# A decoder's state-space scans, prepared by halves and beside the first attention

## The chip, the cores and the metric

The kernel runs on one core of one Trainium2 chip. A core has five engines with a queue of instructions each: TensorE (PE, matmuls and transposes; PEld is its loading of weights), VectorE (DVE), ScalarE (ACT), GpSimd (POOL) and SyncE (SP, which issues the DMA transfers). Each engine works through its own queue in order; engines wait for one another through semaphores. The metric is the device time of one execution in microseconds (us).

## The reference

A decoder of four layers works on `x` of 4 x 256 x 256 (batch, positions, width), with a context of 4 x 256 x 128. Each layer is three parts, and after each part comes `x = layernorm(x + part(x))`: twelve parts in all. The change touches the first six at most:

- **First attention** (16 query heads of 128 that share one key and value head, causal, rotary positions).
- **First state-space part.** Its scan depends on the *context* alone; `x` only enters through the gate:

```python
x = jnp.einsum('ed,bld->bel', in_proj_w, hidden_states)   # the context
xc = conv of 4 taps over the positions of x, per channel
u = silu(xc + conv_b)
dt, Bm, Cm = split(x_proj_w @ u)                          # 8, 16 and 16 rows
delta = softplus(dt_proj_w @ dt + dt_proj_b)
state = state * exp(delta * A) + (delta * u) * B_t        # 16 states, 256 positions
y = sum over states of state * C_t, + D * u
out = y * silu(z)                                         # z is the decoder's x
```

- **First feed-forward part ("thought").** The last position of each batch is normed, multiplied by `agg_w`, and goes four times through norm, a 256x1024 matmul, gelu and a 1024x256 matmul. The result is broadcast over the positions, weighed by `sigmoid(x @ gate_w + gate_b)`, added and normed.
- **Second attention** (16 query heads of 16, four key heads), **second state-space part** (of the same form as the first), then a mixture of 32 experts and six more parts.

## The kernel before

`x` is held in SBUF as [128, 8, 256] (8 tiles of 128 positions) and also transposed, `xT`. The parts run one after the other in one program. A scheduler in the build decides the order in each engine's queue from the order in the source, from tile buffers and from priorities, so the order in a queue isn't the source's; the orders spoken of below are read from the built programs.

Since the scans of both state-space parts need only the context, they run beside other parts. `Scans` is a generator. `begin(pre)` starts it for layer "l0x" or "l1x" and runs its preparation, `beside(n)` issues n scan steps, `upto(b)` as many as batch b needs. One layer has 4 batches x 16 states = 64 scan steps over [128, 2, 256], two layers 128. One step issues: a broadcast DMA of B and C for the state (`bc`, 256 KB); two exponentials `dA<-delta,negA` on ACT; the product `s<-du,bc` on POOL (L123); the scan `s<-dA,s` on DVE (L520); the product with C, `s<-s,bc`, on DVE (L111); and one matmul that adds up the states into a PSUM bank, `ssmps<-s,idz` on PE. `s` and `bc` have four buffers, the scans have one PSUM bank ("ssmps"), and this bank serves the preparation too.

The preparation of a layer (`_steps` up to `turn = 0`) is: load the four taps of the convolution and multiply them with the input projection (POOL); four banks of convolution matmuls; Silu over all 2048 columns; for each half (two batches) a matmul to `xd`, two DMAs to `bcd` in DRAM, two matmuls of `dt` with an add on DVE (`delta<-ssmps`) and an Abs on ACT (`du<-ssmps`); then Exp and Ln over all 2048 columns, and for each of two channel halves `delta<-delta,du` on DVE (L120) and `du<-delta,u` on POOL.

The first attention, `run_mqa`, has 32 steps n, 8 for each batch. A step issues `shares(n)` (reciprocals and scaling of the weights p), `scores(n+1)`, `queries(n+4)` (into the bank `pm`, tag "mm"), two scan steps, `turn(n)` (transposes of p), `output(n-1)` (acc<-oT) and `sums(n)` (o and oT). After the eighth step of a batch the accumulator is added to x (`x<-acc`), and the norm follows. `gate_pair(b)` finishes the first state-space part for one batch: Silu of x, product with y, two transposes, add to x, norm.

`run_thought` prepares its weights, makes the gates (8 pairs of matmuls and one Sigmoid), runs the chain of the last positions and the loop of four turns (each with one `rstd<-ps`), reads the result (`lastmean`), and goes through the gated tail. `run_gqa` is the second attention: 8 projections with one scan step each, then 32 steps of `SmallHeads.run` with one each.

Of the kernel before, what the change touches and what calls it, by code (L numbers as in the profile page):

```python
# [231 lines left out]
def run_mqa(K, w, more):  # L232
    nc, tc = K.nc, K.tc
    with ExitStack() as ctx:
# [121 lines left out]

        N = 8 * B
        keys(0)
# [9 lines left out]
        for n in range(N):  # L368
            shares(n)
            if n + 1 < N:  # L370
                scores(n + 1)
            if n + 4 < N:
                queries(n + 4)
            if n in (2, 3, 4, 5):
                rest.pop(0)()
            if n == 6:
                more()
            K.scans.beside(2)
            turn(n)
            if n:  # L380
                output(n - 1)
            sums(n)
            if n % 8 == 2 and n > 8 and K.fused(0):
                gate_pair(K, wk, y, n // 8 - 1)
        output(N - 1)
        if K.fused(0):
            gate_pair(K, wk, y, B - 1)
            K.scans.begin("l1x")
# [9 lines left out]
class Scans:  # L398
    def __init__(self, K, ctx):
        tc = K.tc  # L400
        self.K = K
        self.one = ctx.enter_context(tc.tile_pool(name="ssm1", bufs=1))
        self.wk = ctx.enter_context(tc.tile_pool(name="ssm2", bufs=4))
        self.ps = ctx.enter_context(tc.tile_pool(name="ssmp", bufs=1, space=PSUM))
        self.dram = ctx.enter_context(tc.tile_pool(name="ssmd", bufs=2, space=bass.MemoryType.DRAM))

        self.dA = [self.one.tile([P, DC, L], F32, name=f"dA{k}") for k in range(3)]
        for t in self.dA:
            K.nc.gpsimd.memset(t[:, :, 0:1], 0.0)
        self.w = {}  # L410
        self.left = iter(())
        self.done = 0

# [12 lines left out]
    def begin(self, pre):  # L426

        self.left = self._steps(pre)
        self.done = 0
        next(self.left)  # L430
# [11 lines left out]
    def _steps(self, pre):  # L442
        K, nc, w, wk = self.K, self.K.nc, self.w[pre], self.wk
        cols = w["cols"]
        N = B * L
        u = self.one.tile([P, DC, N], F32, name="u", bufs=2)
        delta = self.one.tile([P, DC, N], F32, name="delta")
        du = self.one.tile([P, DC, N], F32, name="du")
# [3 lines left out]
        for j in range(4):  # L452
            t = wk.tile([P, D], F32, name="tap", tag="bc", padded_shape=[P, 2 * L])
            nc.sync.dma_start(out=t, in_=K.A[f"{pre}_cw"][:, j * D : (j + 1) * D].to_broadcast([P, D]))
            K.ptt(t, t, w["in"], MUL)
            taps.append(t)
        for h in range(2):
            for c in range(DC):
                ps = self.bank()
                for j in range(4):  # L460
                    K.mm(ps, taps[j][:, c * P : (c + 1) * P], K.ctxp[:, 2 * h : 2 * h + 2, j : j + L], j == 0, j == 3)
                K.act(u[:, c, 512 * h : 512 * h + 512], ps, AF.Identity, bias=cols[:, c, 0:1])
        K.act(u, u, AF.Silu)
        negA = self.one.tile([P, DC, 16], F32, name="negA")
        K.act(negA, cols[:, :, 2:18], AF.Exp)
        K.ts(negA, negA, -1.0, None, MUL)
        bc = self.dram.tile([2, 16, N], F32, name="bcd")
        for h in range(2):
            s = slice(512 * h, 512 * h + 512)
            xd = wk.tile([P, 512], F32, name="xd", tag="s")  # L470
            ps = self.bank()
            for c in range(DC):
                K.mm(ps[0:40, :], w["xp"][:, c, :], u[:, c, s], c == 0, c == DC - 1)
            nc.scalar.copy(xd[0:40, :], ps[0:40, :])
            for k in range(2):
                nc.sync.dma_start(out=bc[k, :, s], in_=xd[8 + 16 * k : 24 + 16 * k, :])
            for c in range(DC):
                ps = self.bank()
                K.mm(ps, w["dt"][:, c * P : (c + 1) * P], xd[0:8, :])

                K.ts(delta[:, c, s], ps, cols[:, c, 1:2], None, ADD)
                K.act(du[:, c, s], ps, AF.Abs, bias=cols[:, c, 1:2])
        K.act(du, du, AF.Exp, scale=-1.0)
        K.act(du, du, AF.Ln, bias=K.eps[1.0])
        for c in range(DC):
            K.stt(delta[:, c, :], delta[:, c, :], 0.0, du[:, c, :], MAX, ADD)
            K.ptt(du[:, c, :], delta[:, c, :], u[:, c, :], MUL)

        turn = 0
        self.y = u  # L490
# [4 lines left out]
        def add(b, n, s):  # L495
# [4 lines left out]
            if n == 15:  # L500
                for c in range(DC):
                    v = u[:, c, b * L : (b + 1) * L]
# [3 lines left out]
        for b in range(B):  # L506
            lo = b * L
            for n in range(16):
                yield
                if len(late) > 1:  # L510
                    add(*late.pop(0))
                t = wk.tile([P, 2, L], F32, name="bc", tag="bc")
                nc.sync.dma_start(out=t, in_=bc[:, n, lo : lo + L].unsqueeze(0).to_broadcast([P, 2, L]))
# [20 lines left out]
def gate_pair(K, pool, y, b):  # L534

    K.scans.upto(b)
# [3 lines left out]
    K.ptt(gate, gate, y[:, :, b * L : (b + 1) * L], MUL)  # L540
# [7 lines left out]
def run_gate(pre):  # L548


    def run(K, w, more):
# [3 lines left out]
        with ExitStack() as ctx:  # L555
            wk = ctx.enter_context(K.tc.tile_pool(name="gate1", bufs=2))
            ctx.enter_context(K.turns())
            for b in range(B):
                gate_pair(K, wk, y, b)
# [25 lines left out]
def run_thought(K, w, more):  # L585
# [4 lines left out]
    with ExitStack() as ctx:  # L590
# [82 lines left out]

        gate = one.tile([P, NT, D], F32, name="gate")
        for i in range(NT):
            ps = pm.tile([P, D], F32, name="ps", tag="mm")
            for c in range(DC):
                K.mm(ps, K.xT[:, c, i * P : (i + 1) * P], w["gate"][:, c, :], c == 0, c == DC - 1)
            K.tt(gate[:, i, :], ps, row["gate_b"], ADD)
        K.act(gate, gate, AF.Sigmoid)  # L680

# [15 lines left out]
        ct = centred(th, B)  # L697

# [49 lines left out]
        K.scans.beside(24)  # L748
# [233 lines left out]
def run_gqa(K, w, more):  # L982
    nc, tc = K.nc, K.tc
    more()
    with ExitStack() as ctx:
# [46 lines left out]
        if K.fused(3):  # L1032
            heads16.then = lambda b: gate_pair(K, wk, K.scans.y, b)
# [1404 lines left out]
```

## Time and profile before

| | |
|---|---|
| median of 3 runs | 2505.26 us (2502.23 to 2517.76) |
| profiled execution | 2505.99 us, its span 2504.2 us |
| mean granted PE clock | 0.939 |
| PE, DVE, ACT, POOL busy | 2277.2, 1460.8, 802.4, 530.6 us |
| first scan, last scan of the second layer | 88.6 and 771.4 us |
| last x<-acc of the first attention | 393.7 us |
| first rstd of the thought loop, lastmean | 442.2 and 519.6 us |
| last norm of the thought's tail | 567.7 us |
| first exponential, last norm of the second attention with its gates | 623.1 and 799.4 us |

Times in the profile are counted from the span's start. A line of a timeline has the start, the duration in us, the engine, the line of the kernel, the operation, output<-inputs, their shapes and the count; in brackets stands the idle time of the engine just before it and what ended it. Line numbers can be those of a helper (L111 is `tt`, L115 `ts`, L120 `stt`, L123 `ptt`, L126 `act`, L132 `mm`). The table of windows gives busy time and, in brackets, the number of instructions for each engine, then the granted PE clock, the share of the DMA engines and GB/s. The page's slices are 40 equal parts of the span, each digit the busy share in tenths.

### The profile page before, as it was taken

To read this page: it belongs to the slowest core of one execution; us is meant where nothing else is said; L and a number is where in the kernel's file an instruction comes from. 1 tells how busy PE (TensorE), PEld (TensorE's weight loads), DVE (VectorE), ACT (ScalarE), POOL (GpSimd) and SP (SyncE) were. 2 spreads that over 40 slices of the span, in tenths; PEclk is the share of its full clock that TensorE was granted. 3 is DMA by queue.
4 is the path that set the end of the run, shared out by engine and by line. 5 is a ranking of instruction groups with operands and counts; after the bars stand their busy time and mean duration, and the time that the engine had idled before them with its cause. 6 is when DMAs were issued, how large, how long until landed. Compare 5 with 4: busy or idle time off the path is not lost. (4 is left out here: it accounts for less than half of the span.)

```text
span 2504.2 us, 28859 instructions
## 1 busy us (share of the span) xinstructions
PE 2277.2 (91%) x10624; PEld 1526.3 (61%) x10624; DVE 1460.8 (58%) x2824; ACT 802.4 (32%) x1781; POOL 530.6 (21%) x617
## 2 busy tenths in 40 slices
PE   8798988648996999989999999999999989799997
PEld 5466654224443565545888888888776544476774
DVE  3798984588875412182356454444555667774556
ACT  3566663422442111153111111111122244343434
POOL 2544543663332222210001100011110002100001
PEclk9899999677987999999999999999988899999999
DMA  5221221122223254230123111211100002100000
GB/s 197 60 60 45 57 54 40 41 61 42 52 46 109 88 158 130 66 112 29 45 66 110 48 58 45 71 46 47 46 22 1 20 18 70 40 1 1 1 1 17
DMA packets 132836, 138.99 MB, mean 56 GB/s; under 512 B 13876, under 2 KB 120726, under 8 KB 130904
## 3 DMA queue, kind: packets, MB, share of 16 engines
q1 hardware_dynamic: 132696, 137.16, 19.1%
q8 instruction: 84, 1.38, 0.2%
q14 instruction: 56, 0.46, 0.1%
HBM read 134.27 MB, written 2.85 MB: 55 GB/s over the span
## 5 line engine op out<-in xcount | busy, mean ns | idle before, releaser
L132 PE MATMUL ps<-xw,xcT 128*128 128x256 f32 (+1 forms) x2304 | 519.0, 382 | 0.3 <-ACT YT L126 0.3
L132 PEld LDWEIGHTS ps<-xw,xcT 128*128 128x128 f32 x2304 | 430.7, 190 | 64.2 <-issue 1.9
L132 PE MATMUL sc<-kT,qT 32*128 32x256 f32 (+2 forms) x1024 | 240.7, 412 | 11.1 <-DVE qn L129 10.7
L520 DVE TENSOR_TENSOR_SCAN s<-dA,s 128x512 f32<-128x512 f32 x128 | 210.3, 1666 | 35.6 <-POOL s L123 35.4
L123 POOL TENSOR_TENSOR s<-du,bc 128x512 f32<-128x512 f32 x128 | 178.9, 1410 | 231.0 <-PE ssmps L132 191.1
L132 PEld LDWEIGHTS sc<-kT,qT 128*128 128x128 f32 (+1 forms) x1024 | 152.9, 206 | 92.3 <-issue 57.8
L132 PE MATMUL ssmps<-s,idz 128*128 128x512 f32 x256 | 147.1, 683 | 33.6 <-DVE s L111 33.5
L111 DVE TENSOR_TENSOR xp<-ps,xb 128x256 f32<-128x256 f32 x96 | 40.4, 421 | 227.0 <-PE ps L132 224.8
L126 ACT ACTIVATE dA<-delta,negA 128x255 f32<-128x255 f32 x256 | 117.7, 501 | 160.5 <-DVE s L520 160.3
L126 ACT ACTIVATE p<-sc,nm 128x256 f32<-128x256 f32 (+1 forms) x256 | 112.1, 445 | 109.5 <-DVE nm L129 103.7
L111 DVE TENSOR_TENSOR hT<-u,a 128x512 f32<-128x512 f32 x48 | 33.2, 691 | 186.1 <-PE u L132 186.1
L132 PE MATMUL o<-pT,vt 128*128 128x256 f32 (+1 forms) x352 | 121.1, 467 | 21.9 <-ACT pT L332 21.5
L123 POOL TENSOR_TENSOR xp<-xp,rn 128x128 f32<-128x128 f32 x96 | 35.2, 402 | 476.9 <-DVE rn L1406 476.9
L169 POOL TENSOR_SCALAR rstd<-mv 128x2 f32<-128x2 f32 x48 | 12.2, 255 | 551.3 <-DVE mv L161 541.4
L126 ACT ACTIVATE sq<-xp 128x1024 f32<-128x1024 f32 x24 | 25.4, 1057 | 314.3 <-DVE xp L111 314.2
L129 DVE TENSOR_REDUCE qn<-sc 128x2 f32<-128x480 f32 (+1 forms) x192 | 87.2, 506 | 43.6 <-PE sc L132 42.9
L129 DVE TENSOR_REDUCE nm<-sc 128x2 f32<-128x512 f32 (+1 forms) x128 | 77.2, 613 | 49.8 <-PE sc L132 49.2
L126 ACT ACTIVATE e<-sT 128x512 f32<-128x512 f32 x128 | 70.1, 591 | 108.3 <-PE sT L132 107.8
L1474 DVE TENSOR_TENSOR_SCAN dec<-xT,idz 128x256 f32<-128x256 f32 (+1 forms) x192 | 89.8, 537 | 25.0 <-DMA xT<-ad 25.0
L111 DVE TENSOR_TENSOR s<-s,bc 128x512 f32<-128x512 f32 x128 | 103.6, 829 | 1.1
L123 POOL TENSOR_TENSOR hT<-hT,sel 128x512 f32<-128x512 f32 x48 | 60.7, 1268 | 202.1 <-DVE hT L111 102.6
L132 PE MATMUL sT<-q,kT 32*128 32x256 f32 (+1 forms) x384 | 96.4, 502 | 1.7 <-ACT e L126 1.5
(503 smaller groups left out, 4067.1 us busy)
## 6 DMA issues: line engine op xcount, KB each, us to landing
bc<-bcd SPq DMA_DIRECT2D x128, 256.0 KB, 4.6
xw<-in_l2a_xw_dram SPq DMA_DIRECT2D x24, 768.0 KB, 4.9
xT<-ad SPq DMA_DIRECT2D x12, 1024.0 KB, 4.5
wj<-in_l1f_gate_dram SPq DMA_DIRECT2D x48, 128.0 KB, 2.6
wj<-in_l1f_up_dram SPq DMA_DIRECT2D x48, 128.0 KB, 3.1
wj<-in_l1f_down_dram SPq DMA_DIRECT2D x48, 128.0 KB, 3.5
sel<-cwd SPq DMA_DIRECT2D x32, 192.0 KB, 3.0
sel<-cwd SPq DMA_DIRECT2D x32, 128.0 KB, 3.5
```

The source lines that it names most:

```text
L111: self.nc.vector.tensor_tensor(out=out, in0=a, in1=b, op=op)
L123: self.nc.gpsimd.tensor_tensor(out=out, in0=a, in1=b, op=op)
L126: self.nc.scalar.activation(out, in_, func, **kw)
L129: self.nc.vector.tensor_reduce(out=out, in_=in_, axis=AX.X, op=op, **kw)
L132: self.nc.tensor.matmul(out, lhsT=lhsT, rhs=rhs, start=start, stop=stop)
L169: self.nc.gpsimd.tensor_scalar(out=out, in0=in_, scalar1=add, scalar2=None, op0=ADD)
L520: nc.vector.tensor_tensor_scan(out=s.rearrange("p c l -> p (c l)"), data0=dA.rearrange("p c l -> p (c l)"), data1=s.rearrange("p c l -> p ...
L1474: nc.vector.tensor_tensor_scan(out=dec[:, k, h, :], data0=ap[:, h, at(bb, k, j) : at(bb, k, 2)], data1=K.idz[:, 0 : (2 - j) * P], initial=0.0,
```

## The change

The preparation becomes a generator of its own, `prepare(pre, bank)`, with 13 yields, which goes by halves of two batches: each half has its own tiles u, delta and du, and its chain is run to its end before the second half's begins. Silu is applied to each bank of the convolution, Exp and Ln to each half. The product du = delta * u moves from POOL to DVE. The taps get tiles of their own, one buffer each, which both layers use. The first layer's preparation uses the scans' bank as before. The second layer's uses the attention's bank "mm", and three of its pieces are issued in each of the attention's last four steps; the rest follows the last `output`. After that eight scan steps are issued, and 32 instead of 24 ahead of the thought's tail. The gates of the first three batches come at n % 8 == 5 instead of 2. In `run_thought` the gates' matmuls come after the chain's start. `upto` moves from `gate_pair` to its callers.

```diff
@@ run_mqa
         N = 8 * B
+        bank = lambda: pm.tile([P, 512], F32, name="ps", tag="mm")
+        ahead = K.scans.prepare("l1x", bank)
...
             sums(n)
-            if n % 8 == 2 and n > 8 and K.fused(0):
-                gate_pair(K, wk, y, n // 8 - 1)
+            if K.fused(0):
+                if n % 8 == 5 and n > 8:
+                    gate_pair(K, wk, y, n // 8 - 1)
+
+                if n + 4 >= N:
+                    for _ in range(3):
+                        next(ahead)
         output(N - 1)
         if K.fused(0):
+            K.scans.upto(B - 1)
+            for _ in ahead:
+                pass
+            K.scans.start("l1x")
             gate_pair(K, wk, y, B - 1)
-            K.scans.begin("l1x")
+            K.scans.beside(8)
@@ Scans
     def begin(self, pre):
-        self.left = self._steps(pre)
+        for _ in self.prepare(pre, self.bank):
+            pass
+        self.start(pre)
...
-    def _steps(self, pre):
+    def prepare(self, pre, bank):
...
-        u = self.one.tile([P, DC, N], F32, name="u", bufs=2)
-        delta = self.one.tile([P, DC, N], F32, name="delta")
-        du = self.one.tile([P, DC, N], F32, name="du")
...
         for j in range(4):
-            t = wk.tile([P, D], F32, name="tap", tag="bc", padded_shape=[P, 2 * L])
+            t = self.one.tile([P, D], F32, name=f"tap{j}")
...
         for h in range(2):
+            u, delta, du = (self.one.tile([P, DC, 2 * L], F32, name=n, bufs=3) for n in ("u", "delta", "du"))
+            halves.append((u, delta, du))
             for c in range(DC):
-                ps = self.bank()
+                ps = bank()
                 for j in range(4):
                     K.mm(ps, taps[j][:, c * P : (c + 1) * P], K.ctxp[:, 2 * h : 2 * h + 2, j : j + L], j == 0, j == 3)
-                K.act(u[:, c, 512 * h : 512 * h + 512], ps, AF.Identity, bias=cols[:, c, 0:1])
-        K.act(u, u, AF.Silu)
+                K.act(u[:, c, :], ps, AF.Silu, bias=cols[:, c, 0:1])
+            yield
...
+                K.ts(delta[:, c, :], ps, cols[:, c, 1:2], None, ADD)
+                K.act(du[:, c, :], ps, AF.Abs, bias=cols[:, c, 1:2])
+            yield
+            K.act(du, du, AF.Exp, scale=-1.0)
+            K.act(du, du, AF.Ln, bias=K.eps[1.0])
+            yield
+            for c in range(DC):
+                K.stt(delta[:, c, :], delta[:, c, :], 0.0, du[:, c, :], MAX, ADD)
+                K.tt(du[:, c, :], delta[:, c, :], u[:, c, :], MUL)
+                yield
-        for c in range(DC):
-            K.stt(delta[:, c, :], delta[:, c, :], 0.0, du[:, c, :], MAX, ADD)
-            K.ptt(du[:, c, :], delta[:, c, :], u[:, c, :], MUL)
@@ run_thought
-        gate = one.tile([P, NT, D], F32, name="gate")
-        for i in range(NT):
-            ps = pm.tile([P, D], F32, name="ps", tag="mm")
-            ...
-        K.act(gate, gate, AF.Sigmoid)
-
         last = K.tp.tile([B, D], F32, name="last", tag="tp")
...
         ct = centred(th, B)
+
+        gate = one.tile([P, NT, D], F32, name="gate")
+        for i in range(NT):
+            ...
+        K.act(gate, gate, AF.Sigmoid)
...
-        K.scans.beside(24)
+        K.scans.beside(32)
```

## The prediction

> **What bounds the kernel now.** I read the page's slices first, because the change touches only the first layer and the start of the second: from the experts of the second layer on, each engine's instruction order is the same in both built programs.
>
> ```profile
> PE   8798988648996999989999999999999989799997
> DVE  3798984588875412182356454444555667774556
> ```
>
> A slice is 62.6 us. TensorE (PE) is 80 to 90% busy nearly everywhere; its two low stretches in the first 800 us are slices 7 to 9 (438 to 563 us), the thought loop and its gated tail. VectorE (DVE) is nearly full in slices 3 to 5, half empty in slices 1, 7 and 8. So two engines take turns as the bound, and the scans, which are DVE work, are the load that can be moved. Next, a table of windows cut at the kernel's own marks: first scan, last x<-acc of the attention, first rstd of the thought loop, lastmean, last norm of the tail, first exponential and last norm of the second attention.
>
> ```profile
> core 0: us, PE busy (x) PEld busy (x) DVE busy (x) ACT busy (x) POOL busy (x), PEclk, DMA share, GB/s
> 88.00:394.00 306.00, 267.42 (x1096) 182.38 (x1097) 265.12 (x340) 186.32 (x529) 150.12 (x108) 0.94 0.22 54
> 394.00:442.00 48.00, 40.75 (x142) 21.09 (x141) 19.63 (x42) 18.49 (x26) 20.21 (x39) 0.89 0.18 45
> 442.00:520.00 78.00, 47.62 (x223) 19.77 (x223) 52.64 (x51) 40.32 (x70) 45.89 (x33) 0.72 0.24 54
> 520.00:568.00 48.00, 19.13 (x46) 9.65 (x47) 40.68 (x85) 7.51 (x17) 29.73 (x33) 0.65 0.20 45
> 568.00:623.00 55.00, 49.83 (x193) 27.79 (x193) 46.05 (x90) 13.36 (x36) 20.18 (x38) 0.78 0.23 48
> 623.00:799.00 176.00, 156.52 (x971) 71.74 (x967) 128.98 (x191) 70.90 (x133) 53.38 (x53) 0.87 0.23 53
> ```
>
> In the first attention both engines are close to full (267 and 265 of 306 us). In the tail DVE is the bound (40.7 of 48), in the second attention PE (156.5 of 176). Between 394 and 442 DVE works only 19.6 of 48 us. The DVE timeline says why: no scan is ready.
>
> ```profile
> 382.87 0.69 DVE L111 TENSOR_TENSOR s<-s,bc 128x512 f32<-128x512 f32 x1
> ...
> 393.69 0.76 DVE L111 TENSOR_TENSOR x<-acc,x 128x256 f32<-128x256 f32 x2 [6.12 <-PE acc L132]
> ...
> 458.25 2.36 DVE L120 SCALAR_TENSOR_TENSOR delta<-delta,du 128x1024 f32<-128x1024 f32 x2 [9.45 <-ACT du L126]
> ...
> 467.37 2.27 DVE L520 TENSOR_TENSOR_SCAN s<-dA,s 128x512 f32<-128x512 f32 x1 [1.00 <-POOL s L123]
> ```
>
> The 64th scan's product ends at 383.6 and the 65th scan starts at 467.4: 84 us in which the second layer's scans are being prepared (394 to 465, 71 us) and none runs. The 46 left after the thought loop (128 scans less the 82 ahead of lastmean) lie in the tail, the projections and the second attention, where they compete for the bound.
>
> **The change, part by part.** The profiled execution took 2505.99 us (span 2504.2), the median is 2505.26; I sum against 2506.
>
> *One scan step* costs DVE 1.666 us (mean of 128 scans, 1.185 to 2.298) and 0.829 for the product with C, PE one 512-column matmul. On PE,
>
> ```profile
> 358.51 1.88 PE L132 MATMUL ssmps<-s,idz 128*128 128x512 f32 x4
> 360.23 0.60 PE L330 MATMUL ps<-idz,p 128*128 128x128 f32 x4
> ```
>
> four records are two matmuls, 1.72 us between the starts, so 0.86 us each. Beside the second attention the same matmul takes 0.96 to 1.12 us.
>
> *What the orders say.* By the count of scans ahead of each mark on DVE, before and after: last x<-acc 64 and 65; first rstd 64 and 81; lastmean 82 and 106; end of the tail 88 and 110; the second attention gets 29 before and 15 after, the 15 inside its first half. So the move does take place; the question is what each window pays.
>
> *First scan.* It waits for half a preparation instead of a whole one. Before: products of delta at 80.3, then 5.6 us of POOL for du, first scan at 88.6. After, by the same rows shifted: first half's delta at about 62, but the four tap products for the second layer now stand on POOL ahead of the first s, behind the second half's convolution (65) and a 2.9 us DMA; with 4 x 0.72 and s at 1.3 the scan starts near 73.5. The 15 us are not all gain: 6.4 us of DVE work that stood ahead of the first scan now stands behind it.
>
> *Last x<-acc of the attention, 393.7 before.* DVE's bound: 265.1 + 6.4 + one more scan and product 2.5 + the second preparation 8.0 (four adds of 0.75, four 0.6, four products of 0.65 that POOL had) = 282 us of work; with the 33 to 41 us of waits that this window has now, 73.5 + 282 + 33..41 = 388 to 397. The attention's own bound: step 28's o matmul stands at 364.3; with three scans fewer ahead of it and one gate put off I place it at 350. From there to the last x<-acc before took 28.3; the preparation puts 24 matmuls into it, 24 x 0.86 = 20.6, and 3 us of waits: 52, so 402. The later bound holds: **402 (+8)**, ends 388 and 412.
>
> This is where eight more table loads fall into ACT's queue (23 before in the first two layers, 37 after: Silu, Exp and Ln now change by halves between the attention's exponentials). They are in the 52 at nothing beyond the 3 us, because ACT works 186 of 306 us here; queued behind a load are the step's Exp, then its transposes, o and oT. The row:
>
> ```profile
> 431.56 0.69 ACT L126 ACTIVATE du<-ssmps,w_l1x_cols 128x512 f32<-128x512 f32 x1 [2.29 <-DVE delta L115]
> 432.26 1.28 ACT L126 ACT_TABLE_LOAD   x1
> 433.56 1.91 ACT L126 ACTIVATE gate<-gate 128x2048 f32<-128x2048 f32 x1
> ```
>
> A load is 1.28 us and the next activation starts 0.02 us after it. Uncovered, eight cost 8 x 1.28 = 10 us; that is the upper end, 412. The Trainium skill speaks against the change here: "ScalarE: Activation LUTs", section "What ACT_TABLE_LOAD costs", prices a switch of tables at the load plus a drain of about the same length, some 2.66 us. The row shows the load and no such drain around it. By the page, an estimate, eight uncovered switches would be 21 us and x<-acc would come near 423; I go by the row.
>
> *x<-acc to first rstd, 48.5 before.* DVE had 19.6 us of work here; now it gets 16 scans, 16 x 2.5 = 40, with the rest 61.3. At 0.92 busy, as in the attention's undisturbed steps (18.6 of 20 us), 66; ends 62 (full) and 72 (0.85, the tail's share). The eight pairs of gate matmuls leave for the time behind the first chain, which is hidden by PE's idle time (7 of 48 here, 30 of 78 in the loop). **66 (+17.5)**: the new scans stand in front of the loop's start.
>
> *Thought loop, 77.4 before.* 25 scans instead of 18, but preparation (delta, du; 3.0 + 2.4) and waits gone: DVE 64.6 at 0.9, **72 (-5)**. Its chain of small matmuls and norms needs its own time; two of its four turns take 18.3 and 17.8 us with scans beside them, 4 x 17.5 = 70 is the lower end.
>
> *Tail, 48.1 before:* DVE 40.7, of which 7 scans; after 4, 7.5 us less, and 1.5 of waits: **39 (-9)**.
>
> *Projections, 55.4:* DVE 46 with 9 scans, 33 with 3 or 4; PE works 49.8 at a clock of 0.78, of which 6 scans' matmuls: **44 (-11)**, PE's bound.
>
> *Second attention, 176.3:* PE at 0.89 is the bound. 14 or 15 scans fewer, 0.96 to 1.12 us of PE and, where DVE holds the pair of steps, 1.91 us of DVE: 14 x 0.96 = 13 to 15 x 1.91 = 29. I take 1.3 for each, nearer to PE, **157 (-19)**; ends 166, as DVE has slack in the half without scans, and 147.
>
> The marks become 402, 468, 540, 579, 623, 780, against 393.7, 442.2, 519.6, 567.7, 623.1, 799.4. The last mark comes 19 us earlier and nothing behind it changes: 2506 - 19 = **2487**.
>
> **Rivals.** *The preparation hides in the last four steps.* For: PE idles 13% of the window, ACT 39%. Against: both bounds lie above 388. Then x<-acc at 388 (-14 from mine) and, with scans ready sooner, the second attention at 150 (-7): 2466.
>
> *The one bank in the last four steps holds up the attention (slower).* Attention and preparation share one PSUM bank and ACT's in-order queue. Each of the 12 fills must be read by ACT before the next, while a step's queue waits. The preparation alone took 71 us in 394 to 465; if nothing of it lies beside the last four steps, x<-acc comes at 350 + 28 + 71 = 449, 47 later than mine: 2487 + 47 = 2534. It eats the whole gain from x<-acc at 421, and costs 1% from 446. For: every fill of the scans' bank in 394 to 465 waits (2.3 us ahead of the activation shown). Against: half of the 71 us was the thought's start in between.
>
> *Nothing gained.* DVE's work is the same but for du (8 x 0.65 = 5.2 us taken over from POOL), and moves to windows where DVE binds: x<-acc at its upper end is +10, 72 for 66 to the first rstd +6, 166 for 157 in the second attention +9: 2512. *The change does not do what it says* is out: the counts above move.
>
> **How the numbers follow.** A measurement of this kernel tells about 1% (25 us) from no change. Chances: my forecast 0.43 (2470 to 2505), hidden 0.25 (2450 to 2475), nothing gained 0.15 (2505 to 2520), the one bank 0.17 (2515 to 2560). Faster than 2480: four fifths of the second case and a third of the first, 0.35. Slower than 2531: two thirds of the last and a little of the others, 0.14. Best ends together (388, 62, 147) give 2506 - 19 - 14 - 4 - 10 = 2459; 8 in 10 lie from 2456 to 2530.
>
> **What would show it.** Right: first scan near 73; x<-acc near 402; scans between x<-acc and the first rstd with DVE above 0.9; second attention near 157 with its last scan in the middle. Wrong: gaps on PE ahead of steps 28 to 31's o, ended by ACT or by the bank; a first scan at 80 or later; a second attention that is not shorter by 13 us, which would mean that its scans were free where they were.

## The result, and the profile after

| | before | changed |
|---|---|---|
| median of 20 runs | 2507.16 us (2496.72 to 2524.73) | 2516.28 us (2503.97 to 2533.01) |
| ratio | 1 | 1.0027, interval 1.0005 to 1.0049 |
| profiled execution, span, PE clock | 2505.99, 2504.2, 0.939 | 2510.20, 2508.4, 0.939 |

The changed kernel is 0.27% slower, some 7 us, where 0.8% faster was forecast. The measured median lies in the range that was given, on the other side of no change.

The page's slices of the changed kernel (62.7 us each; slice 0 is the first) show DVE at seven tenths in slices 6 and 7, 376 to 502 us, where it had four and five, and PE at 7, 5, 7 and 6 tenths in slices 6 to 9, where only 7 and 8 had been low:

```profile
PE   7898997576997899989999999999999989799997
...
DVE  4788967788673512173355444444565667774556
```

The table of windows of the changed kernel, cut at the same marks as before (first scan, last x<-acc, first rstd, lastmean, end of the tail, first exponential, last norm):

```profile
core 0: us, PE busy (x) PEld busy (x) DVE busy (x) ACT busy (x) POOL busy (x), PEclk, DMA share, GB/s
69.00:410.00 341.00, 306.76 (x1202) 201.63 (x1200) 278.00 (x362) 220.45 (x584) 152.73 (x107) 0.93 0.21 51
410.00:472.80 62.80, 36.81 (x125) 18.97 (x126) 53.92 (x77) 28.16 (x53) 35.24 (x36) 0.76 0.35 81
472.80:559.60 86.80, 56.04 (x242) 23.21 (x241) 69.70 (x65) 39.98 (x74) 57.39 (x46) 0.80 0.34 74
559.60:595.00 35.40, 14.79 (x36) 8.36 (x36) 29.32 (x76) 4.83 (x11) 23.49 (x33) 0.60 0.12 30
595.00:643.00 48.00, 44.36 (x183) 25.62 (x185) 36.45 (x81) 8.55 (x25) 13.85 (x38) 0.78 0.14 30
643.00:812.30 169.30, 151.79 (x939) 70.19 (x937) 98.58 (x159) 58.60 (x103) 32.44 (x38) 0.82 0.14 31
```

The stretch from 394 to 442, in which DVE had 19.6 of 48 us of work, is filled: 53.9 of 62.8. What was gained in the tail (12 us), the projections (8) and the second attention (6) was paid with 16 us up to the last x<-acc, 14.5 to the first rstd, and 9.4 in the loop. The last norm comes 13.6 us later than before; the order of the instructions from there on is the same, and 9.4 of the 13.6 us went away again in this one execution.

**How much of a difference between two executions is the clock.** The 119 runs of the kernel before beside the experiments have mean granted clocks of 0.926 to 0.944 and times of 2498 to 2530 us. A straight line through them falls 1.8 us for each 0.001 of clock and leaves 2.3 us of scatter. At a clock of 0.935 this line gives 2513.1 us for the kernel before and 2520.8 for the changed one, so +7.7. Below, "at equal clock" means this comparison: the mean distance of a kernel's runs from the line through the runs of the kernel before that stand beside it. By the scatter of its own 9 to 20 runs such a mean is good to 1 us or less. It stands beside the ratios, not in their place, since a kernel can also change the clock that it gets.

### The profile page after: what moved, and what is told of

The parts are those of the page before. It is cut to its first block, busy times and chain, and to the rows that moved or that the text cites. A ratio compares the mean times of both kernels' runs of the same rounds, so it can differ in the third digit from the quotient of the medians.

```text
span 2508.4 us, 28875 instructions
## 1 busy us (share of the span) xinstructions
PE 2279.3 (91%) x10624; PEld 1525.0 (61%) x10624; DVE 1467.8 (59%) x2836; ACT 818.3 (33%) x1797; POOL 523.1 (21%) x613
## 5 line engine op out<-in xcount | busy, mean ns | idle before, releaser
L132 PE MATMUL sc<-kT,qT 32*128 32x256 f32 (+2 forms) x1024 | 235.0, 400 | 10.7 <-DVE qn L129 10.1
L132 PE MATMUL ssmps<-s,idz 128*128 128x512 f32 x256 | 154.2, 716 | 60.4 <-DVE s L111 42.1
L123 POOL TENSOR_TENSOR xp<-xp,rn 128x128 f32<-128x128 f32 x96 | 35.2, 406 | 476.9 <-DVE rn L1440 476.9
L126 ACT ACTIVATE sq<-xp 128x1024 f32<-128x1024 f32 x24 | 25.4, 1057 | 314.1 <-DVE xp L111 314.1
L132 PEld LDWEIGHTS ssmps<-s,idz 128*128 128x128 f32 x256 | 50.2, 217 | 106.9 <-DVE s L111 56.9
```

Of the source, the lines that this page charges most:

```text
L123: self.nc.gpsimd.tensor_tensor(out=out, in0=a, in1=b, op=op)
L126: self.nc.scalar.activation(out, in_, func, **kw)
L132: self.nc.tensor.matmul(out, lhsT=lhsT, rhs=rhs, start=start, stop=stop)
```

## The experiments

The marks of the profiled executions, in us: when the last x<-acc of the attention stands, and the length of each stretch behind it (norms by their start). Each row is one execution, and the clock moves single stretches: halves_only and halves_gate5, with the same five scans in the projections, took 48.7 us there at a clock of 0.89 and 54.5 at 0.72. So a difference of some 6 us in one stretch of two rows shows nothing by itself.

| kernel | last x<-acc | to first rstd | loop | tail | projections | second attention | ratio to before (interval) | at equal clock |
|---|---|---|---|---|---|---|---|---|
| before | 393.7 | 48.5 | 77.4 | 47.4 | 56.1 | 175.6 | 1 | 0 |
| changed | 409.8 | 63.0 | 86.8 | 35.3 | 48.1 | 169.3 | 1.0027 (1.0005-1.0049) | +7.7 |
| gates_back | 405.5 | 50.2 | 89.4 | 34.8 | 58.3 | 166.8 | 0.9998 (0.9976-1.0021) | +2.3 |
| no_gx | 404.3 | 64.9 | 75.8 | 37.1 | 47.1 | 167.7 | 0.9986 (0.9959-1.0013) | +3.1 |
| no_gx_gates_back | 405.9 | 53.0 | 80.2 | 36.2 | 55.4 | 170.5 | 0.9974 (0.9950-0.9997) | +0.8 |
| late_gates_back | 380.7 | 61.6 | 88.4 | 53.3 | 61.1 | 171.0 | 1.0041 (1.0015-1.0067) | +11.2 |
| no_gx_late | 384.4 | 52.8 | 88.0 | 52.9 | 57.0 | 169.0 | 1.0002 (0.9980-1.0025) | +4.9 |
| halves_only | 388.2 | 51.8 | 80.2 | 35.3 | 48.7 | 176.6 | 0.9947 (0.9919-0.9975) | -12.9 |
| halves_gate5 | 380.9 | 55.9 | 79.5 | 35.2 | 54.5 | 174.9 | 0.9938 (0.9909-0.9966) | -15.7 |
| halves_du_pool | 388.0 | 51.8 | 82.0 | 35.4 | 47.1 | 176.4 | 0.9935 (0.9901-0.9970) | -8.9 |
| halves_8_32 | 388.1 | 67.6 | 88.5 | 53.3 | 61.1 | 167.7 | 1.0083 (1.0056-1.0110) | +20.7 |
| no_gx_8_32 | 392.1 | 60.9 | 86.9 | 52.4 | 57.2 | 170.8 | 1.0068 (1.0046-1.0090) | +11.2 |
| halves_no_gx | 387.7 | 58.8 | 81.3 | 37.8 | 47.6 | 173.9 | 0.9974 (0.9946-1.0002) | -1.8 |

### The moved gate matmuls

In the changed kernel's loop the first turn, from one `rstd<-ps` to the next, takes 30.6 us (472.80 to 503.44), the next two 18.1 and 17.6. The timelines of POOL, DVE and PE in this turn:

```profile
478.95 2.33 POOL L123 TENSOR_TENSOR gx<-gate,r_l0f_rows 128x256 f32<-128x256 f32 x2
...
491.25 1.41 POOL L123 TENSOR_TENSOR gx<-gx,x 128x256 f32<-128x256 f32 x2
492.61 2.49 POOL L123 TENSOR_TENSOR s<-du,bc 128x512 f32<-128x512 f32 x2
```

```profile
493.91 4.71 DVE L549 TENSOR_TENSOR_SCAN s<-dA,s 128x512 f32<-128x512 f32 x1 [9.35 <-POOL s L123]
```

```profile
499.40 2.08 PE L132 MATMUL ssmps<-s,idz 128*128 128x512 f32 x2 [11.05 <-DVE s L111]
501.27 0.85 PE L132 MATMUL ps<-pick,add 128*128 128x4 f32 x4
```

`gx` (gate * bc_b + x for the tail) can start once the Sigmoid is through, now inside the loop. For 13.7 us POOL has no s to give, so DVE runs out of scans and idles 9.35 us; and the matmul of the scan that is missing stands in PE's queue ahead of `pick`, which the loop itself needs. The loop waits for a scan that waits for work of the tail. Two ways to take this away, alone and together (no_gx computes the same sum in another order):

```diff
 gates_back: run_thought
+        gate matmuls, adds and Sigmoid (as in the kernel before)
         last = K.tp.tile([B, D], F32, name="last", tag="tp")
...
         ct = centred(th, B)
-        gate matmuls, adds and Sigmoid
 no_gx: run_thought
-            K.ptt(gx[:, i, :], gate[:, i, :], row["bc_b"], MUL)
-            K.ptt(gx[:, i, :], gx[:, i, :], K.x[:, i, :], ADD)
...
-                K.mm(ps, thT[...], w["bc"][:, c, :], c == 0, c == DC - 1)
+                K.mm(ps, thT[...], w["bc"][:, c, :], c == 0, False)
+            K.mm(ps, K.ident, row["bc_b"], False, True)
...
-                K.ptt(gate[:, i, :], gate[:, i, :], gx[:, i, :], ADD)
+                K.ptt(gate[:, i, :], gate[:, i, :], K.x[:, i, :], ADD)
```

> The changed kernel with one part undone: the thought's eight pairs of gate matmuls and the Sigmoid stand ahead of the chain of the last positions again. Theory (the moved gates hold up the thought): in the changed kernel the first rstd waits for gate matmuls that PE takes one by one as DVE's adds come free between scans (456 to 472 us), and POOL's gx products, which need the Sigmoid, stand in one block of 13.7 us (479 to 492.6) ahead of s in the loop's first turn, which takes 30.6 us instead of 18. With the gates back the first turn should take 18 to 20 us, x<-acc to lastmean 150 -> 130 to 138 us, and the kernel 10 to 18 us less than the changed one: 0.996 to 0.999 of the kernel before. Rival (DVE's work alone counts, and it is the same): x<-acc to lastmean stays at 146 to 152, the ratio at 1.002 to 1.004.

> The changed kernel without the 16 gx operations on POOL: bc_b is added by one more matmul for each batch into the bank that the gates are multiplied with (4 matmuls of 0.4 to 0.9 us), and x is added in place of gx; the orders of scans around the marks stay the same. Theory (POOL's gx block holds up the scans, and a scan's matmul in PE's queue holds up the loop): the loop's first turn falls from 30.6 to 18 to 20 us, lastmean minus first rstd from 86.8 to 74 to 77, and the kernel is 8 to 13 us faster than the changed one: 0.998 to 0.9995 of the kernel before. Rival (25 scans in the loop fill DVE, whatever POOL does): the loop stays at 83 to 88 us and the ratio within 0.001 of the changed kernel's.

> The run with the gates back, again without the gx operations on POOL. Theory: the 8.7 us in which DVE and PE wait for POOL in the loop's first turn go, the loop takes 78 to 82 us instead of 89, and the kernel 6 to 10 us less than the run with the gates back: 0.996 to 0.9975 of the kernel before, faster than both. Rival: within 3 us of the run with the gates back.

Without gx on POOL, and nothing else changed, the turn is 19.5 us (469.22 to 488.77) and the loop 75.8 instead of 86.8:

```profile
469.22 0.14 DVE L115 TENSOR_SCALAR rstd<-ps 128x4 f32<-128x4 f32 x1
...
488.77 0.15 DVE L115 TENSOR_SCALAR rstd<-ps 128x4 f32<-128x4 f32 x1
```

Six scans start in this turn in both. So the block is the cause of the long turn, 11 us. With the gates back the stretch ahead of the loop gives 12.8 us. Not all of it is the eight matmul pairs that no longer stand between the chain's start and the first rstd: only 11 scans lie in this stretch instead of 16, and at the 1.6 us that a scan costs there (next section) the missing five are 8 us, an estimate. The loop stays at 89.4, since there too the gx block ran inside its first turn (POOL, 456 to 471), which takes 24.7 us where 18 to 20 were expected. Of the whole kernel gates_back wins 5.4 us at equal clock, where 10 to 18 were expected, and no_gx 4.6, where 8 to 13 were; their ratios' intervals overlap that of the changed kernel. It is less than either stretch shows, because the scans move along: with the gates back 7 of them lie in the projections instead of 3, which take 58.3 us instead of 48.1. Both together (no_gx_gates_back) take the loop to 80.2, as expected, but at equal clock the kernel is only 1.5 us below gates_back, the rival's answer.

### What a scan costs beside each part

```diff
 before_bare (kernel before), after_bare and after_none (changed): Scans, gates of the second attention
-        for b in range(B):
+        for b in range(B if pre == "l0x" else n):    # n = 2, 3, 0
...
-    K.scans.upto(b)                                  # in the second attention's gates
```

before_bare and after_bare leave out 32 and 16 of the second layer's 64 scan steps, after_none all of them.

> The kernel before without the second layer's last two batches of scans (32 of 64 scan steps left out): nothing runs beside the second attention. Forecast's price (1.3 us for each scan beside the second attention): the 176 us from the first exponential to the last norm become 138 (29 x 1.3 = 38 less). Theory (the scans are almost hidden there, at 0.4 to 0.8 us each): 153 to 164 us.

> The changed kernel without the second layer's last batch of scans (16 of 64 left out). Forecast's price: the 170 us from the first exponential to the last norm become 150 (15 x 1.3). Theory (0.4 to 0.8 us each): 158 to 164. If the two bare kernels differ in this stretch by more than 3 us, something other than scans (the granted PE clock at its start) differs between the two kernels there.

> The changed kernel without any of the second layer's scan steps (its preparation stays). It gives what each stretch takes without scans. Theory: x<-acc to first rstd 45 to 50 us (63 with 16 scans), loop 64 to 70 (86.8 with 25), tail 28 to 31 (35.3 with 4), projections 40 to 46 (48.1), second attention 145 (169.3 with 15). So scans cost 0.5 to 0.8 us each ahead of and in the loop, 1.6 in the second attention's first half. Forecast: DVE is the bound in the first two (61 and 65 us of DVE work with scans): without scans 48 and 60.

Without scans the second attention takes 146.0 and 145.5 us, 29.6 and 23.8 less: 1.0 us for each of the 30 that the trace has there, 1.6 for each of 15. The whole kernels, by the mean of all runs at equal clock, are 25.6 us faster for 32 scans and 15.6 for 16, so 0.8 to 1.0 each; the profiled execution of after_bare lay 6 us below the mean of its runs. My new theory of almost hidden scans fell, and the forecast's 1.3 was about right as a mean. What was wrong is that the mean holds for those that were taken out. The second attention cut in quarters (eight of its steps each), first the third and fourth quarter of the kernel before, with 8 and 5 scans:

```profile
708.58:751.63 43.05, 38.47 (x230) 16.31 (x226) 33.90 (x50) 19.24 (x37) 14.68 (x13) 0.88 0.23 47
751.63:783.43 31.80, 27.91 (x186) 11.78 (x186) 20.07 (x33) 13.37 (x23) 9.74 (x10) 0.95 0.11 24
```

The same two of the changed kernel, which has no scans there:

```profile
730.93:763.64 32.71, 30.85 (x218) 14.35 (x220) 15.95 (x30) 12.67 (x20) 3.13 (x5) 0.90 0.00 1
763.64:795.75 32.11, 27.89 (x175) 10.98 (x176) 9.83 (x20) 11.49 (x18) 3.13 (x5) 0.79 0.00 1
```

And the fourth quarter of before_bare, the kernel before with these scans left out:

```profile
718.62:750.72 32.10, 27.89 (x175) 10.98 (x176) 9.83 (x20) 11.49 (x18) 3.12 (x5) 0.79 0.00 1
```

Eight scans of the third quarter were worth 10.3 us in this pair, 1.3 each. The five of the fourth were worth nothing: PE is busy 27.9 us with and without them, at a clock of 0.95 with and 0.79 without. The other executions settle this. Counted to the last exponential, the fourth quarter took 28.0 to 28.2 us at a clock of 0.94 in all five with five or six scans there, and 28.0 to 28.6 us at 0.73 to 0.76 in all eleven without. The third is less even: 43.0 to 43.2 us with eight scans, 32.3 to 37.2 at clocks of 0.77 to 0.89 without, so 0.7 to 1.4 each. The first quarter, with 9 scans in both, took 45.6 us at a clock of 0.79 against 41.4 at 0.88; in gates_back it took 41.3 at 0.89. So of 15 scans taken out 2 belonged to the second quarter (1.7 us), 8 to the third, 5 were free where they were, and 4 us went to the lower clock of the first quarter in this execution.

In the loop the scans are dearer. Without any it takes 41.7 us and the stretch ahead of it 37.6, below what I expected (64 to 70 and 45 to 50), and the loop does so at a clock of 0.54, against 0.80 in the changed kernel. 25 scans cost the loop without gx 34 us, 1.4 each; in the kernel before 18 scans and what is left of the preparation cost 35.7. Where the tail has 10 instead of 4 (below), it is 18 us longer, 3 each. after_none is one execution; at equal clock it lies some 100 us below the changed kernel, 1.6 us for each scan in all. The 16 scans ahead of the loop cost 25.4 us, 1.6 each. Only the last quarter of the second attention hides them.

### Halves alone, and with one more part of the change each

halves_only takes from the change the preparation by halves, with the taps' own tiles and du on DVE, and leaves the rest as before: preparation of the second layer behind the attention through the scans' bank, gates at step 2, gate matmuls ahead, 24 scans ahead of the tail. The others differ from it by one edit:

```diff
 halves_8_32
             K.scans.begin("l1x")
+            K.scans.beside(8)
...
-        K.scans.beside(24)
+        K.scans.beside(32)
 halves_gate5
-            if n % 8 == 2 and n > 8 and K.fused(0):
+            if n % 8 == 5 and n > 8 and K.fused(0):
 halves_du_pool
-                K.tt(du[:, c, :], delta[:, c, :], u[:, c, :], MUL)
+                K.ptt(du[:, c, :], delta[:, c, :], u[:, c, :], MUL)
 halves_no_gx
 the edit of no_gx
```

> The preparation by halves alone: the second layer's preparation starts behind the first attention through the scans' own bank, gates at step 2, gate matmuls ahead of the thought's chain, 24 scans ahead of the tail. Theory: the first scan at 67 to 69 us and the last x<-acc at 380 to 384 (12 us earlier than before); the second layer's scans start about 35 us behind it instead of 71; the second attention has its 29 scans and its 176 us again. 8 to 15 us faster than the kernel before, 0.994 to 0.997. Rival (what is gained in the attention is lost at scans' price further on, as in the run without early preparation): 0.999 to 1.004.

> The run with halves alone, and one more part of the change: 8 scan steps issued behind the first attention and 32 instead of 24 ahead of the thought's tail. In the built order this alone moves the second layer's scans: 109 instead of 94 stand ahead of the projections, 15 instead of 29 are left for the second attention. Theory (a scan costs 1.4 to 2 us in the loop and the tail, and 0 to 1.3 in the second attention's second half, where the moved ones come from): lastmean to first exponential grows from 84 to 105 to 115 us, the second attention falls from 176.6 to 169 to 172, and the kernel is 12 to 22 us slower than with halves alone: 0.999 to 1.004 of the kernel before. Rival (the forecast's price, 1.3 us for each scan taken out of the second attention, PE's bound): as fast as halves alone or up to 8 us faster, 0.991 to 0.995.

> The run with halves alone, and the 16 gx operations of POOL replaced by a matmul for each batch. Theory: the loop's first turn, 24.7 us with 3 scans beside it, falls to 15 to 18 us and the kernel to 4 to 9 us less than with halves alone: 0.991 to 0.9935 of the kernel before, the fastest of all. Rival (the time saved in the turn is taken by scans that move in): within 3 us of halves alone.

> The run with halves alone, and the gates of the first three batches at step 5 instead of 2. The scans' order around the marks is the same. Theory: the last x<-acc comes 5 to 8 us earlier (380.7 in the run without early preparation, which had the gates at step 5, against 388.2), and this is all: 0.992 to 0.995 of the kernel before. Rival (order of three gates doesn't matter, the 7 us were the clock): x<-acc at 386 to 390, the ratio that of halves alone within 0.0015.

> The run with halves alone, and du = delta * u on POOL again instead of DVE. Theory (it is the halves that bring the gain): first scan 1 to 3 us later (a half's du takes 2 x 1.4 us of POOL), DVE has 2.6 us less in each preparation; the time within 4 us of halves alone, 0.993 to 0.9965 of the kernel before. Rival (du on DVE is the gain): 0.998 or more.

**Halves alone are the good part**: 0.9947, 13 us faster than before. The attention ends 5.5 us earlier, where 10 to 14 were expected, and the second layer's scans start 48 us behind its last x<-acc instead of 74. Tail and projections are 12 and 7 us shorter (the 7 at a clock of 0.89 against 0.78), and the second attention keeps its scans and its time. The scans do move: 88 instead of 82 lie ahead of lastmean, five of the six in the loop, which grows by 2.9 us; tail and projections have 4 and 5 instead of 7 and 9. Gates at step 5 bring the last x<-acc to 380.9, 7.2 us earlier, as expected; in that execution the stretch ahead of the first rstd and the projections are longer by 4.1 and 5.8, at clocks of 0.80 and 0.72 against 0.88 and 0.89, and the whole kernel is at 0.9938. With du on POOL the first scan comes at 67.4 us as it does without (67.5), not 1 to 3 later; the ratio is 0.9935 and the time at equal clock 4 us longer. The two measures disagree, so no difference is shown. halves_gate5 is, with halves_du_pool, the fastest kernel of this study, 0.6% below the kernel before and some 0.9% below the changed one.

**The counts 8 and 32 are the bad part**: from 0.9947 to 1.0083, 34 us at equal clock, more than the theory's 12 to 22. This is with the second layer's preparation behind the attention; with it early, the changed kernel has only 4 scans in its tail. They move 16 scans from the second attention, which wins 8.9 us, into the loop (5 scans, +8.3 us), the tail (6, +18), the projections (3, +12.4, at a clock of 0.75 instead of 0.89) and the stretch ahead of the first rstd (2). That stretch grows by 15.8 us, and 12.7 of these are one DVE operation. The timeline of DVE in halves_8_32:

```profile
429.87 14.02 DVE L117 TENSOR_SCALAR r<-tok,tmv,trstd 4x256 f32<-4x256 f32 x1 [0.98 <-POOL trstd L123]
443.92 0.86 DVE L111 TENSOR_TENSOR r<-r,r_l0f_rows 4x256 f32<-4x256 f32 x2
```

and of POOL:

```profile
429.81 3.72 POOL L123 TENSOR_TENSOR s<-du,bc 128x512 f32<-128x512 f32 x3
433.50 1.39 POOL L123 TENSOR_TENSOR gx<-gate,r_l0f_rows 128x256 f32<-128x256 f32 x2
...
443.02 0.71 POOL L123 TENSOR_TENSOR gx<-gx,x 128x256 f32<-128x256 f32 x1
```

An operation on 4 x 256 elements, 0.40 us in the kernel before, takes 14.02, from 0.06 us after POOL begins three s and 15 gx without a gap until 0.16 us after POOL's last.

halves_no_gx missed: its first turn is 21.1 us where 15 to 18 were expected, and at equal clock it is 11 us slower than halves_only, not 4 to 9 faster.

### The early preparation, and the stall

late_gates_back is gates_back with the second layer's preparation behind the last output, through the scans' own bank. no_gx_8_32 and no_gx_late are halves_8_32 and late_gates_back with the edit of no_gx.

```diff
 late_gates_back: run_mqa
-        ahead = K.scans.prepare("l1x", bank)
+        ahead = K.scans.prepare("l1x", K.scans.bank)
...
-                if n + 4 >= N:
-                    for _ in range(3):
-                        next(ahead)
```

> As the run with the gates back, and the second layer's preparation undone too: none of it in the attention's last four steps, all of it behind the last output, through the scans' own bank. Theory (the four steps are full, so the preparation only moves its time): the last x<-acc comes at 386 to 392 instead of 410, x<-acc to lastmean grows by 12 to 20 us as scans start late, and the time is within 6 us of the run with the gates back. Rival 1 (early preparation is a real gain, since DVE gets scans sooner): 10 us or more slower than the run with the gates back. Rival 2 (one bank and ACT's table loads cost more than the early scans bring): 10 us or more faster.

> The run with halves and 8 and 32 scan steps, without POOL's gx operations; the order of scans is nearly the same. In the run with gx a DVE operation on 4x256, r<-tok, takes 14.02 us instead of 0.40 and ends 0.16 us after POOL's block of three s and 15 gx. Theory (DVE's operation can't go on while POOL works without a gap): r<-tok takes 3.5 to 4 us (three s are left), x<-acc to first rstd falls from 67.6 to 55 to 59, the loop's first turn from 30.7 to 18 to 22, and the kernel is 14 to 24 us faster than with gx: 0.999 to 1.003 of the kernel before. Rival (r<-tok waits for something else, and the stretch is bound by scans): r<-tok stays above 10 us or the stretch within 4 us of 67.6.

> The run with the second layer's preparation behind the attention and the gates back, without POOL's gx operations. Beside the run with early preparation and the gates back, also without gx (2514 us at a mean clock of 0.935), it shows what early preparation through the attention's bank brings without the 14 us stall that stood in the first pair. Theory (the stall made the late one slow; early preparation brings nothing or less): 6 us faster to 3 us slower than that run, 0.995 to 0.999 of the kernel before. Rival (early preparation is worth the 8.6 us that the first pair showed): 6 us or more slower, above 1.0.

In the attention the early preparation costs 24.8 us (405.5 against 380.7), and behind it 31.7 us come back up to the second attention's first exponential; in the pair without gx it is 21.4 and 25.9. The first pair makes it worth 8.9 us at equal clock, where less than 6 was expected. But late_gates_back has the same stall as halves_8_32 (r<-tok 14.00 us). With gx gone, r<-tok takes as long as POOL's three s:

```profile
437.27 3.81 DVE L117 TENSOR_SCALAR r<-tok,tmv,trstd 4x256 f32<-4x256 f32 x1 [0.98 <-POOL trstd L123]
441.11 0.86 DVE L111 TENSOR_TENSOR r<-r,r_l0f_rows 4x256 f32<-4x256 f32 x2
```

That is no_gx_8_32; its POOL is busy with s from 437.21 to 440.93. So the stall is POOL's, and no_gx_8_32 is 9.5 us faster than halves_8_32 at equal clock, where 14 to 24 were expected (the ratios' intervals overlap). The stretch ahead of its loop falls from 67.6 to 60.9 us, not to 55 to 59, and the first turn stays at 30.3 where 18 to 22 were expected: nine scans start in it, DVE is busy 27.7 of the 30.3 us, and no block is needed. Without the 14 us on either side early preparation is worth 4.1 us at equal clock (+0.8 against +4.9), between theory and rival. Up to 3.4 of these are still the stall: r<-tok takes 3.81 us in no_gx_late and 0.39 in no_gx_gates_back. The two ratios' intervals overlap, so early preparation by itself is worth little or nothing.

## Why the prediction was wrong

The marks of the changed kernel ran 32 us behind the forecast's by the end of the second attention: +8 at the last x<-acc, -3 to the first rstd, +15 in the loop, -4 in the tail, +4 in the projections, +12 in the second attention. Two steps failed, in the loop and in the second attention.

**First scan, first attention.** The first scan came at 68.9 instead of 73.5, behind the taps' products as forecast. The price of the preparation in the last four steps, 24 matmuls and 3 us of waits, 23.7 us, was right: 24.8 measured by gates_back against late_gates_back, 21.4 by the same pair without gx. The attention ends at 380.7 in late_gates_back (I had 350 + 28.3 = 378). The eight table loads, which the trace has between 357 and 402, are in it: beside 20.6 us of matmuls they and all waits took 4.2 in the first pair, where I had 3 and, at the upper end, 10. The last x<-acc stands at 409.8 in the changed kernel and at 404 to 408 in its siblings with the same order up to there, against 402. It was a small miss, 2 to 8 us. The figure that the Trainium skill gives for a switch of tables ("ScalarE: Activation LUTs", "What ACT_TABLE_LOAD costs") would make the eight loads 21 us, an estimate; no run here left so much room for them.

**To the first rstd.** 63.0 against 66, in part by luck: I held DVE to be the bound, with 61.3 us of work at 0.92 (the terms named, 19.6 + 40, give 59.6), and it worked 53.9 of 62.8, 0.86. The gate matmuls take part. With the gates back the same stretch takes 50.2, but with 11 scans instead of 16, so the share of each isn't separated.

**The thought loop.** 72 forecast, 86.8 measured, the largest miss. The step that failed is "the eight pairs of gate matmuls leave for the time behind the first chain, which is hidden by PE's idle time". I looked for cover on PE and asked what the matmuls cost; I did not follow who waits for their result. It is the Sigmoid, then 13.7 us of gx on POOL, ahead of the s of every further scan. no_gx showed 11 us of it. The few us left fit DVE's work: 66.8 us in 75.8, not 64.6 at 0.9.

**Tail and projections.** 35.3 and 48.1 against 39 and 44: right within what the clock moves.

**Second attention.** 157 forecast, 169.3 measured, 12 us. The price of a scan was right as a mean (1.0 to 1.6), but the step "14 or 15 scans fewer", 1.3 for each, took the mean for all. The ones that went were those of the second half: 1.3 each in the third quarter (0.7 in other executions), 0 in the fourth. My reason for the end of 166, "DVE has slack in the half without scans", isn't what the quarters show: in the last one PE is busy 27.9 us with the scans and without, at the higher clock with them. 4 us more are the clock of the first quarter in this execution; the siblings' second attentions took 167 to 171.

**Rivals.** That nothing is gained (2512) is what happened, though not by its sum: x<-acc (+8) and the second attention (+12) came as it says, the first rstd did not, and the loop isn't in it. The one bank in the attention's last steps did not hold it up (x<-acc 8 us from the forecast, not 47).

**Slips of the working.** PE's low slices are 7 and 8 when the first is slice 0; DVE's are counted from 1. The trace has 89 scans ahead of the tail's end and 30 in the second attention, not 88 and 29. The 28.3 us of the attention's bound count from the end of the o matmul, 364.3 is its start. None of these changes the forecast by more than 2 us.

**The frame.** All of it rested on one picture: 84 us without a scan on DVE are room, and what is moved into them is won further on. after_none shows that the room is not free. The loop takes 41.7 us without scans and is stretched by 1.4 to 2 us for each scan put beside it; taken out of the second attention they save 0 to 1.6. Those that leave the tail save more, 3 each there. The gain of the change comes from another part, halves; that it is less work ahead of the first scan and shorter waits is argued, not tested part by part.

From the kernel before to the changed one the runs make a ladder at equal clock: halves -12.9 us; counts 8 and 32 +33.6 (halves_8_32); gates at step 5 and the last gate issued behind the preparation -9.5 (late_gates_back); early preparation -8.9 (gates_back); gate matmuls moved +5.4; in all +7.7. A rung's worth depends on the rungs below: step 5 alone was worth 2.8 on halves_only, and early preparation 4.1 without gx.

What stays open: why no_gx, which wins 9 us on halves_8_32 and 6 on late_gates_back, loses 11 us at equal clock on halves_only (+7 us ahead of the first rstd; 2.5 of them are r<-tok, 3.80 us beside three s instead of 1.35 beside one). Early preparation together with the counts 0 and 24 was not run; in the built order more than 100 scans stand ahead of the second attention even then.

## What to carry to other kernels

Idle time of an engine next to a chain of short dependent steps isn't free room: price it by the stretch's length with the filler taken out. When a piece of work is moved, follow its result to the last consumer and look at what else is queued there; here an operation moved on PE cost its time on POOL. And when work is taken out of a stretch, its worth is that of those instructions at that place, not the mean over the stretch.

## What the runs showed of the hardware

**A short DVE operation can wait for a whole train of POOL's.** r<-tok took 14.02 and 14.00 us where POOL had 18 operations back to back (halves_8_32, late_gates_back), 3.81 in no_gx_8_32 and no_gx_late, where it had three, 1.35 in halves_only, where it had one, and 0.40 in the kernel before, where it had none. A scan that started in POOL's train of four s in the changed kernel (492.61 to 497.54) took 4.71, where no other of its 128 took over 2.3, and ended 1.1 us after the train. The Trainium skill ("SBUF — State Buffer", section "SBUF: two separate sides") has DVE, for some forms of its operations, and GpSimd share a pair of ports by an exclusive lock that is held for a whole instruction. The runs agree that r<-tok as the loser stops entirely, and show more: between POOL's back-to-back instructions it did not get in. Other DVE operations did. In the changed kernel, beside the gx block:

```profile
480.76 1.07 DVE L111 TENSOR_TENSOR s<-s,bc 128x512 f32<-128x512 f32 x1
481.75 1.74 DVE L549 TENSOR_TENSOR_SCAN s<-dA,s 128x512 f32<-128x512 f32 x1
```

```profile
481.24 2.78 POOL L123 TENSOR_TENSOR gx<-gx,x 128x256 f32<-128x256 f32 x2
```

Both engines went on, slower: 1.07 us for a product that elsewhere takes 0.69, and 2.78 us for two gx that take 1.41 later in the block. What decides which operation gets in was not tested.

**The granted clock decides several us in a comparison.** In the records PE can be busy without a pause and still be at half clock. The windows of the changed kernel at the end of the last quarter:

```profile
778.00:782.00 4.00, 1.40 (x5) 0.87 (x6) 2.14 (x6) 2.99 (x4) 1.26 (x1) 0.90 0.00 0
782.00:786.00 4.00, 4.00 (x8) 1.25 (x7) 1.45 (x6) 1.18 (x2) 0.93 (x2) 0.50 0.00 0
786.00:790.00 4.00, 4.00 (x33) 1.38 (x32) 0.00 (x0) 0.60 (x1) 0.00 (x0) 0.50 0.00 0
```

After 2.6 us of idle time PE is full for 8 us at a clock of 0.50. In the kernel before the five scans stand there and the clock of the quarter is 0.95; with the scans left out (before_bare) it is 0.79. So the scans kept the clock up and paid their own time by it; that it was their matmuls, and not another part of a scan, is argued, not tested by itself. The same second attention without any scan took 145.4 us at a clock of 0.86 (after_bare) and 162.9 at 0.74 (after_none).
